# A macaron block with 4-bit weights: VectorE and DMA turn the down results and the convolution's rows

## The chip, the cores and the metric

The kernel runs on one core of one Trainium2 chip. The metric is the device time of one execution in microseconds (us), as the median of several runs. A separate execution, taken by the hardware profiler, gives the rows that are quoted below. PE is TensorE, DVE is VectorE, ACT is ScalarE, POOL is GpSimd, and SP is the engine that issues most DMAs.

## The reference

The input has 2048 tokens (2 x 1024) of 1024 channels in float32. The block is a feed-forward half step, a state-space convolution, and another feed-forward half step:

```python
x = x + 0.5 * ffn(layernorm(x))
x = x + s4(layernorm(x))
x = x + 0.5 * ffn(layernorm(x))

ffn(x) = (silu(x @ Wg) * (x @ Wu)) @ Wd     # 1024 -> 2752 -> 1024
W[k, n] = scales[k // 128, n] * (w4[k, n] - (z4[k // 128, n] + 1))   # 4 bits each
s4(u)  = causal convolution of u, along its last axis (1024), with a kernel K, plus D * u
```

K is made from the state-space parameters. The convolution runs along the channel axis, independently for each token, and the same K serves all tokens. So it can be written as products with triangular Toeplitz blocks, and the convolved axis has to stand on the partitions for that.

## The kernel before

**Jobs.** The 2048 tokens are cut into 4 blocks b of 512 (TB), and each block into 4 tiles t of 128 rows. Rows of x stand on partitions. A job is one feed-forward step of one block: `JOBS` (L1418) lists the eight as (b, k), where k = 1 is the first and k = 3 the second feed-forward: (0,1), (1,1), (0,3), (1,3), (2,1), (3,1), (2,3), (3,3). Job j runs `gate_up` and then `down`.

**Gate/up** (L727) has 64 steps: 8 waves over the intermediate columns by 8 groups g of 128 input channels. A wave has 6 units (3 column tiles by gate and up) in most waves, 4 in two and 5 in the last, and each unit holds one of the 8 PSUM banks. One step multiplies the group's weights by the block, with a high and a low part of x (two matmuls of 128x512 for each unit, L753). Since the scale differs from group to group, the accumulated bank is rescaled in place after every group: by ACT for even units (L723) and by DVE for odd ones (L725). The next group's products into that bank wait for it.

**Down** (L814) has 44 steps: 2 halves a of the output columns by 22 input tiles f. One step has 4 banks c (128 output channels each, 512 tokens wide) with two matmuls each (L825); banks c0 and c2 are rescaled by ACT, c1 and c3 by DVE. At f = 21 the result goes to four tiles y (L837, from `ypool`, which has 4 buffers). They hold output channels on partitions, so they are turned before they are added to x.

**Turning the down results.** `back(b, a, t)` (L843) takes a PSUM bank, makes four TensorE transposes of 128x128 (L847), one from each y, and DVE adds the bank to x (L849). For a = 0 these stand in steps 26 to 41 of the same down, for a = 1 in steps 0 to 3 of the next job's gate/up.

**The convolution** of the block that the job before finished (when k was 1) stands in the gate/up of jobs 1, 2, 5 and 6. For each of 4 tiles, `norm` makes normalized rows (L223), `swap` (`turn_whole`, L1193) turns them by eight transposes (L230) into PSUM and copies them to SBUF by ACT (L1201) and DVE (L1199), and `convolve` (L1137) makes sums on POOL (L1146 to L1148), small products in two halves with two banks each (L1151), and adds to x on DVE (L1181 to L1191).

**Other work beside it.** The next block's rows are normalized (L256), split by POOL and turned by DMA transposes (`turn_by_dma`, L258) during down. Weights are loaded as bytes on SP's queue four steps ahead (L685 in gate/up, L692 in down, 6 buffers) and cast by POOL three steps ahead (L701, 5 buffers).

**Order.** `at(up, s, f)` and `at(dn, d, f)` put a piece of work in front of step s of gate/up or d of down in the order of writing. A scheduler then orders each engine's instructions by its own estimate; `in_order_of_writing(f, engines)` holds f to the written order on the named engines. `bank()` gives out the 8 PSUM banks in rotation, `acc()` holds one until `give_back`.

Of the kernel before, what the change touches and what calls it, by code (L numbers as in the profile page):

```python
# [55 lines left out]
def macaron_s4_kernel(  # L56
# [785 lines left out]

    def back(b, a, t):  # L843

        ps = bank(f"pb_{b}_{a}_{t}")
        for c in range(4):
            nc.tensor.transpose(ps[:, bass.ts(c, P)], yT[a, c][:, bass.ts(t, P)], ident)  # L847
        part = x[b][t][:, bass.ts(a, 512)]
        nc.vector.tensor_tensor(part, part, ps, ALU.add)  # L849
# [570 lines left out]
    def fast():  # L1420
# [5 lines left out]
        for j, (b, k) in enumerate(JOBS):  # L1426
# [7 lines left out]
            if prev:  # L1434
                pb, pk = prev
                for t in range(NT):
                    at(up, t, lambda t=t: back(pb, 1, t))
                if pk == 1:
                    late = 34 if j == 1 else 0
                    at(up, 4, lambda: moments(pb, 2))  # L1440
                    at(up, 5, lambda: deviations(pb, 2))
                    s4x, s4n = {}, {}

                    def norm(t):
                        s4n[t] = normalized(pb, t)

                    def swap(t):
                        s4x[t] = turn_whole(s4n.pop(t), f"st_{pb}_{t}")
# [19 lines left out]
                    at(up, late + 28, save)  # L1468
                else:
# [6 lines left out]
                    at(up, 4, store)  # L1476
# [21 lines left out]
            if after:  # L1498
# [44 lines left out]
            at(dn, o, lambda: load_x(b, rows_of(u, b) if k == 1 else saved(b)))  # L1543
            for t in range(NT):
                at(dn, o + 5 + gap * t, lambda t=t: back(b, 0, t))
                if not after:
                    first_half = lambda t=t: store_half(t, 0, nc.sync)
                    at(dn, o + 6 + gap * t, first_half)
# [207 lines left out]
```

## Time and profile before

| | |
|---|---|
| median of 3 runs | 2097.34 us (2096.61 to 2097.39) |
| span of the profiled execution | 2095.8 us |
| granted TensorE clock, mean | 0.998 |
| PE busy | 2054.6 us |
| DVE busy | 1671.5 us |
| ACT busy | 1398.9 us |
| POOL busy | 1291.6 us |
| DMA packets | 239719, of which 98747 under 512 B |

The profiled execution has its span, from the first to the last instruction, as its own time; no device time stands beside it. It is 1.5 us under the median of the three runs, which had no profile. "Chain" means the chain of work that ended last, followed back from the last instruction to what released each step. A group is written as line, engine, operation, output and inputs with their shapes, count, then busy time and the mean of one in ns. The durations of neighbouring matmuls overlap, so the chain, not the mean, says what one adds.

### The profile page before, as it was taken

Reading aid. Unit: us, or ns where it says so; the run is one execution under the profiler, and the core shown is the slowest. Engines: PE = TensorE matmul, PEld = TensorE weight load, DVE = VectorE, ACT = ScalarE, POOL = GpSimd, SP = SyncE. Lnnn points to the kernel's source line nnn. Section 1 sums busy time; section 2 is a strip of 40 time slices with the busy share of each in tenths; the row PEclk is TensorE's granted clock in tenths of the full one; section 3 lists DMA queues with packets and bytes.
Section 4 is the critical chain, followed back from the end, with each engine's and each line's share of the span. In section 5 each row is a group of like instructions: output and inputs, shape, how many; then the busy total and the mean of one; then the engine's idle time right before and its main releaser. Section 6 shows DMA issues by size and latency. Waiting matters only on the chain.

```text
span 2095.8 us, 30242 instructions
## 1 busy us (share of the span) xinstructions
PE 2054.6 (98%) x9556; PEld 1410.6 (67%) x9556; DVE 1671.5 (80%) x2749; ACT 1398.9 (67%) x2185; POOL 1291.6 (62%) x1688
## 2 busy tenths in 40 slices
PE   6999999999999999999999999999999999999998
PEld 4555775677776578655876568675686766866576
DVE  8888887778888877797778878878788787777776
ACT  6777777746655776667667776547765467667775
POOL 5867758657754577555955568455684546845542
PEclk9999999999999999999999999999999999999999
DMA  4324321113411126211441124111151111531111
GB/s 144 119 85 146 111 66 54 36 56 74 110 39 55 32 53 170 72 31 36 122 137 37 31 51 126 44 51 32 46 130 37 51 39 35 133 128 36 33 35 60
DMA packets 239719, 151.03 MB, mean 72 GB/s; under 512 B 98747, under 2 KB 226596, under 8 KB 239550
## 3 DMA queue, kind: packets, MB, share of 16 engines
q1 hardware_dynamic: 238246, 146.60, 24.7%
q8 instruction: 78, 1.28, 0.3%
q10 hardware_dynamic: 1016, 1.82, 0.2%
q14 instruction: 91, 0.75, 0.1%
q0 software_dynamic: 288, 0.59, 0.1%
HBM read 104.45 MB, written 25.50 MB: 62 GB/s over the span
## 4 chain that ended last, share of the span: by engine, by line
PE 92%; DVE 4%; DMA 1%; ACT 1%; issue 1%; POOL 0%; SPq 0%; ACTq 0%; DVEq 0%; POOLq 0%
PE pg L753 56%; PE po L825 29%; PE pc L1151 3%; PE pb L847 1%; PE pb L1151 1%; DVE pg L725 1%; PE st L230 1%; DMA b<-wq 1%; ACT g L780 0%; DVE po L725 0%; DVE x L256 0%; DMA x<-in_L_attn_u_dram 0%; POOL q L608 0%; DVE hf L783 0%; PE pt L230 0%
## 5 line engine op out<-in xcount | busy, mean ns | idle before, releaser
L723 ACT ACTIVATE pg<-pg,rat 128x512 f32<-128x512 f32 x1240 | 787.5, 661 | 418.1 <-PE pg L753 415.9
L725 DVE TENSOR_TENSOR pg<-pg,rat 128x512 f32<-128x512 f32 x1168 | 776.6, 693 | 159.3 <-PE pg L753 153.4
L753 PE MATMUL pg<-xTh,w_up 128*128 128x512 f32 x2752 | 840.5, 435 | 1.1 <-DVE pg L725 0.7
L753 PE MATMUL pg<-xTl,w_up 128*128 128x512 f16 x2752 | 716.7, 382 | 11.6 <-DVE pg L725 5.6
L701 POOL CAST w_up<-b 128x768 fp32r<-128x768 int8 (+2 forms) x490 | 378.0, 777 | 504.6 <-PE pg L753 405.7
L753 PEld LDWEIGHTS pg<-xTh,w_up 128*128 128x128 f32 x2752 | 518.3, 189 | 175.9 <-DVE pg L725 12.2
L723 ACT ACTIVATE po<-po,ratd 128x512 f32<-128x512 f32 x660 | 431.8, 661 | 164.7 <-PE po L825 164.1
L825 PE MATMUL po<-hl,w_down 128*128 128x512 f32 x1344 | 530.5, 397 | 3.7 <-DVE po L725 3.6
L825 PE MATMUL po<-hh,w_down 128*128 128x512 f32 x1344 | 521.2, 390 | 0.0
L725 DVE TENSOR_TENSOR po<-po,ratd 128x512 f32<-128x512 f32 x620 | 430.4, 698 | 113.3 <-PE po L825 109.1
L753 PEld LDWEIGHTS <-w_up 128*128 128x128 bf16 x2752 | 228.4, 99 | 330.3 <-issue 151.0
L701 POOL CAST w_down<-bd 128x512 fp32r<-128x512 int8 x352 | 218.4, 624 | 158.5 <-PE po L825 90.4
L825 PEld LDWEIGHTS po<-hl,w_down 128*128 128x128 f32 x1344 | 251.2, 188 | 73.3 <-DVE po L725 12.2
L825 PEld LDWEIGHTS po<-hh,w_down 128*128 128x128 f32 x1344 | 252.6, 188 | 49.0
L787 POOL TENSOR_TENSOR hl<-hf,hh 128x512 fp32r<-128x512 f32 x168 | 217.9, 1297 | 8.0
L783 DVE SCALAR_TENSOR_TENSOR hf<-pg,rat,g 128x512 f32<-128x512 f32 x168 | 123.2, 749 | 49.3 <-ACT g L780 40.4
L780 ACT ACTIVATE g<-pg,rat 128x512 f32<-128x512 f32 x168 | 111.0, 687 | 48.5 <-PE pg L753 32.8
L785 POOL CAST hh<-hf 128x512 fp32r<-128x512 f32 x168 | 106.1, 632 | 55.0 <-PE pg L753 31.0
L282 POOL TENSOR_TENSOR lo<-x,hi 128x512 f16<-128x512 f32 x48 | 62.2, 1296 | 0.0
L187 DVE BATCH_NORM_STATS2 stats<-x 128x6 f32<-128x512 f32 x88 | 60.0, 682 | 0.5
L280 POOL TENSOR_TENSOR mid<-hi,top 128x512 bf16<-128x512 f32 x48 | 56.4, 1174 | 0.0
L296 POOL TENSOR_TENSOR xTh<-turned 128x512 fp32r<-128x512 bf16 x48 | 55.9, 1165 | 0.0
(216 smaller groups left out, 1104.2 us busy)
## 6 DMA issues: line engine op xcount, KB each, us to landing
b<-wq SPq DMA_DIRECT2D x319, 96.0 KB
bd<-wdq SPq DMA_DIRECT2D x336, 64.0 KB
x<-in_L_attn_u_dram SPq DMA_DIRECT2D x30, 512.0 KB
b<-wq SPq DMA_DIRECT2D x128, 64.0 KB
xs<-x SPq DMA_DIRECT2D x16, 512.0 KB
x<-xs SPq DMA_DIRECT2D x16, 512.0 KB
out_dram<-x SPq DMA_DIRECT2D x12, 512.0 KB
b<-wq SPq DMA_DIRECT2D x64, 80.0 KB
```

The lines of the kernel that those rows point to most:

```text
L187: nc.vector.bn_stats(stats[:, t, i, :], x[b][t][:, bass.ts(i, 512)])
L282: nc.gpsimd.tensor_tensor(lo[:, own], n[:, own], hi[:, own].bitcast(F32), ALU.subtract)
L701: nc.gpsimd.tensor_copy(t, b)
L723: nc.scalar.activation(dst, src, AF.Copy, scale=sc)
L725: nc.vector.tensor_tensor(dst, src, sc.to_broadcast([P, TB]), ALU.mult)
L753: nc.tensor.matmul(p, weights, (lo, hi)[k][:, g, :], start=(g == 0 and not done), stop=(g == GK - 1 and done), skip_group_check=True,)
L780: nc.scalar.activation(g, pg, AF.Silu, scale=rat[:, 2 * f, GK - 1 :])
L783: nc.vector.scalar_tensor_tensor(hf, pu, last, g, ALU.mult, ALU.mult)
L785: nc.gpsimd.tensor_copy(hi, hf)
L787: nc.gpsimd.tensor_tensor(lo, hf, hi.bitcast(F32), ALU.subtract)
L825: nc.tensor.matmul(ps[c], w[:, bass.ts(c, P)], part, start=(f == 0 and k == 0), stop=(f == NF - 1), skip_group_check=True,)
L1151: nc.tensor.matmul(dst, lhsT, rhs, start=start, stop=stop, skip_group_check=True)
```

## The change

Two uses of TensorE transposes go.

The down results: `blocks_out(a, cs)` transposes each y in place in blocks of 32x32 on DVE and writes it to a DRAM tile `y_dram[a]` (256 KB). `rows_in(b, a, t)` reads the rows of tile t back with four DMAs, one for each 32 partitions, each of 512 runs of 32 floats (128 B); the DMA's addresses put the blocks in their turned places. `back` then adds that tile to x, SBUF with SBUF. The last job's a = 1 keeps the products, under the name `back_by_products`. The writes stand at steps 23 and 24 of down (a = 0) and at steps 0 and 1 of the next gate/up (a = 1), held on DVE and SP; the reads follow at 26, 30, 34, 38 of down (29, 32, 35, 38 in job 0) and at 3 to 6 of gate/up, held on SP, and the adds at 29, 33, 37, 41 and at 5 to 8.

The convolution's rows: `norm` transposes the normalized tile in place on DVE (128x1024, blocks of 32x32) and writes 512 KB to one of two DRAM tiles; `swap` reads it with four DMAs of 1024 runs of 128 B. The convolution's steps move by two or three places (in job 1 two less, since `late` is 32 there), so that the way through DRAM lies between them; the moments, deviations and stores beside them move too.

```diff
+    y_dram = [dpool.tile([TB, 512], F32, tag=f"yz{a}", name=f"yz{a}") for a in range(NH)]
+    s_dram = [dpool.tile([P, HID], F32, tag=f"sz{i}", name=f"sz{i}") for i in range(2)]
+    Q = 32
+    def blocks_out(a, cs):
+        for c in cs:
+            y = yT.pop((a, c))
+            nc.vector.transpose(y, y)
+            nc.sync.dma_start(y_dram[a][bass.ts(c, P), :], y)
+    rows_back = {}
+    def rows_in(b, a, t):
+        r = ypool.tile([P, TB], F32, tag="y", name=f"yr_{b}_{a}_{t}")
+        src = y_dram[a].rearrange("(m j) (t b i) -> t b j m i", j=Q, b=P // Q, i=Q)[t]
+        for q in range(P // Q):
+            dst = r[bass.ts(q, Q), :].rearrange("p (m i) -> p m i", i=Q)
+            nc.sync.dma_start(dst, src[q])
+        rows_back[b, a, t] = r
     def back(b, a, t):
+        part = x[b][t][:, bass.ts(a, 512)]
+        nc.vector.tensor_tensor(part, part, rows_back.pop((b, a, t)), ALU.add)
+    def back_by_products(b, a, t):
...
                 pb, pk = prev
+                for i in range(2):
+                    out_ = lambda i=i: blocks_out(1, (2 * i, 2 * i + 1))
+                    at(up, i, lambda out_=out_: in_order_of_writing(out_, ET.DVE, ET.SP))
                 for t in range(NT):
-                    at(up, t, lambda t=t: back(pb, 1, t))
+                    in_ = lambda t=t: rows_in(pb, 1, t)
+                    at(up, 3 + t, lambda in_=in_: in_order_of_writing(in_, ET.SP))
+                    at(up, 5 + t, lambda t=t: back(pb, 1, t))
                 if pk == 1:
-                    late = 34 if j == 1 else 0
-                    at(up, 4, lambda: moments(pb, 2))
-                    at(up, 5, lambda: deviations(pb, 2))
-                    s4x, s4n = {}, {}
+                    late = 32 if j == 1 else 0
+                    at(up, 8, lambda: moments(pb, 2))
+                    at(up, 9, lambda: deviations(pb, 2))
+                    s4x = {}
                     def norm(t):
-                        s4n[t] = normalized(pb, t)
+                        n = normalized(pb, t)
+                        nc.vector.transpose(n, n)
+                        nc.sync.dma_start(s_dram[t % 2], n)
                     def swap(t):
-                        s4x[t] = turn_whole(s4n.pop(t), f"st_{pb}_{t}")
+                        s4x[t] = s = t4(f"st_{pb}_{t}").rearrange("p (c t) -> p c t", c=NC)
+                        src = s_dram[t % 2].rearrange(
+                            "(b i) (c a j) -> a i c b j", i=Q, a=P // Q, j=Q
+                        )
+                        for q in range(P // Q):
+                            dst = s[bass.ts(q, Q)].rearrange("p c (b j) -> p c b j", j=Q)
+                            nc.sync.dma_start(dst, src[q])
...
+                    pinned = lambda f, *e: lambda: in_order_of_writing(f, *e)
                     for t in range(NT):
-                        at(up, late + 8 + 4 * t, lambda t=t: norm(t))
-                        at(up, late + 10 + 4 * t, lambda t=t: swap(t))
-                        at(up, late + 12 + 4 * t, lambda t=t: conv(t))
-                        at(up, late + 13 + 4 * t, lambda t=t: next(parts[t], None))
-                    at(up, late + 27, lambda: moments(pb, 3))
-                    at(up, late + 28, lambda: deviations(pb, 3, LIFT))
+                        at(up, late + 10 + 4 * t, pinned(lambda t=t: norm(t), ET.DVE, ET.SP))
+                        at(up, late + 13 + 4 * t, pinned(lambda t=t: swap(t), ET.SP))
+                        at(up, late + 15 + 4 * t, lambda t=t: conv(t))
+                        at(up, late + 16 + 4 * t, lambda t=t: next(parts[t], None))
+                    at(up, late + 29, lambda: moments(pb, 3))
+                    at(up, late + 30, lambda: deviations(pb, 3, LIFT))
...
-                            d, where = 31 + 2 * t + half, up
+                            d, where = 32 + 2 * t + half, up
...
+            for i in range(2):
+                out_ = lambda i=i: blocks_out(0, (2 * i, 2 * i + 1))
+                at(dn, 23 + i, lambda out_=out_: in_order_of_writing(out_, ET.DVE, ET.SP))
             for t in range(NT):
-                at(dn, o + 5 + gap * t, lambda t=t: back(b, 0, t))
+                d = o + gap * t + (2 if j == 0 else 5)
+                in_ = lambda t=t: rows_in(b, 0, t)
+                at(dn, d, lambda in_=in_: in_order_of_writing(in_, ET.SP))
+                at(dn, d + 3, lambda t=t: back(b, 0, t))
...
         for t in range(NT):
-            back(b, 1, t)
+            back_by_products(b, 1, t)
```

More of the change, by code (lines that the diff above doesn't have):

```diff
@@ L1466, in save @@
                             nc.sync.dma_start(dst, x[pb][t])
-                    at(up, late + 28, save)
+                    at(up, late + 30, save)
                 else:
@@ L1474, in store @@
                         x.pop(pb)
-                    at(up, 4, store)
+                    at(up, 9, store)
             if j == 0:
@@ L1543, in fast @@
             at(dn, o, lambda: load_x(b, rows_of(u, b) if k == 1 else saved(b)))
+            for i in range(2):
+                out_ = lambda i=i: blocks_out(0, (2 * i, 2 * i + 1))
+                at(dn, 23 + i, lambda out_=out_: in_order_of_writing(out_, ET.DVE, ET.SP))
             for t in range(NT):
-                at(dn, o + 5 + gap * t, lambda t=t: back(b, 0, t))
+                d = o + gap * t + (2 if j == 0 else 5)
+                in_ = lambda t=t: rows_in(b, 0, t)
+                at(dn, d, lambda in_=in_: in_order_of_writing(in_, ET.SP))
+                at(dn, d + 3, lambda t=t: back(b, 0, t))
                 if not after:
                     first_half = lambda t=t: store_half(t, 0, nc.sync)
-                    at(dn, o + 6 + gap * t, first_half)
+                    at(dn, d + 4, first_half)
             gate_up(j, b, up)
```

## The prediction

> **What bounds the kernel now.** I read the busy shares first, then the chain that ended last, then this chain piece by piece in two stages, then rows and windows for prices.
>
> The page's head and chain:
>
> ```profile
> span 2095.8 us, 30242 instructions
> PE 2054.6 (98%) x9556; PEld 1410.6 (67%) x9556; DVE 1671.5 (80%) x2749; ACT 1398.9 (67%) x2185; POOL 1291.6 (62%) x1688
> PE 92%; DVE 4%; DMA 1%; ACT 1%; issue 1%; POOL 0%; SPq 0%; ACTq 0%; DVEq 0%; POOLq 0%
> PE pg L753 56%; PE po L825 29%; PE pc L1151 3%; PE pb L847 1%; PE pb L1151 1%; DVE pg L725 1%; PE st L230 1%; DMA b<-wq 1%; ACT g L780 0%; DVE po L725 0%; DVE x L256 0%; DMA x<-in_L_attn_u_dram 0%; POOL q L608 0%; DVE hf L783 0%; PE pt L230 0%
> ```
>
> PE is busy 98% and carries 92% of the chain, and both groups of transposes that the change removes (pb L847, st L230) stand in the chain under their own names. VectorE, which receives the work, is the next engine, at 80%.
>
> The chain piece by piece, in a down stage and in the gate/up of job 2 (start us, us, what):
>
> ```profile
> 540.10 7.30 PE po L825 x32
> 547.41 0.44 PE pb L847 x4
> 547.84 7.33 PE po L825 x32
> ...
> 594.97 0.87 PE st L230 x8
> 595.84 2.91 PE pg L753 x13
> ...
> 601.39 1.75 PE pc L1151 x12
> 603.15 0.22 PE pb L1151 x2
> ```
>
> PE has no gap around the transposes: 0.44 us for four, 0.87 for eight, then products at once. (32 products take 7.3 us, 0.228 each.) A group's mean duration of 275 ns is not its price, since starts overlap: the price is 0.11 us.
>
> **Removed.** 60 groups at L847 by 0.44 us = 26.4 us; 16 tiles at L230 by 0.87 us = 13.9 us. Sum 40.3 us of PE time on the path, where PE never waits long: job 2's gate/up took 188.6 us against some 185 of PE work. The page's L847 and L230 shares (1.4% and 0.7%, some 44 us) agree. Also gone are 16 copies on ACT (L1201, 586 ns) and 16 on DVE (L1199, 680 ns): both beside PE, at nothing, except that the DVE time pays for part of what comes.
>
> The Trainium skill, "TensorE: Matmul & The Clock Gate", Part 4, gives a PE transpose about 275 ns in a kernel; by that the 368 removed would be 101 us, and the chain's pieces overrule it.
>
> **Added on VectorE.** 60 transposes of 128x512 and 16 of 128x1024, an operation that this trace does not show. Bounds: below, the fastest DVE rows of these shapes (0.53 and 0.80 us); above, the same rows at their slowest:
>
> ```profile
> L256 DVE TENSOR_SCALAR x<-x,mv,r x56: 529/540/1480, 248.4 to 1714.4; 128x512 f32<-128x512 f32 x56
> L223 DVE TENSOR_SCALAR xn<-x,mv,r x16: 802/806/1719, 399.1 to 1646.4; 128x1024 f32<-128x1024 f32 x16
> L1199 DVE COPY st<-st x16: 677/680/683, 416.9 to 1663.7; 128x512 f32<-128x512 f32 x16
> L849 DVE TENSOR_TENSOR x<-x,pb x64: 674/677/690, 267.2 to 2088.5; 128x512 f32<-128x512 f32 x64
> ```
>
> I take the plain copy, 0.68 shown; queued back to back such operations follow at some 0.61 us (four L725 in 2.53). For 128x1024 I take 1.1, nearly twice the pitch. The back's add stays one DVE operation; it now reads SBUF twice instead of PSUM once. I leave it at 0.68, bounded by 0.53 and 1.48.
>
> *In down* (8 stages, half a=0): after y at step 21, two transposes each are pinned at steps 23 and 24. The window of one down stage:
>
> ```profile
> core 0: us, PE busy (x) PEld busy (x) DVE busy (x) ACT busy (x) POOL busy (x), PEclk, DMA share, GB/s
> 505.00:540.00 35.00, 35.00 (x160) 28.93 (x159) 26.92 (x40) 24.33 (x37) 31.10 (x42) 1.00 0.60 150
> 2010.00:2050.00 40.00, 40.00 (x178) 33.09 (x177) 30.05 (x44) 28.30 (x43) 16.18 (x26) 1.00 0.14 40
> ```
>
> DVE is idle 8.1 of 35 us: 0.42 us in each 1.82 us step. The burst is 4 x 0.61 = 2.4 us in two steps with 0.8 us spare, so c1 and c3 are rescaled 1.6 us late. The changed order lets PE take c0 and c2 of the next step first, which is 0.9 us of work; 0.8 us remains. 8 x 0.8 = 6.4 us. If PE's run-ahead covers all: 0. Without cover, with 1.48 us each: 8 x 5.1 = 41.
>
> *In gate/up* (7 stages, half a=1): the same burst in steps 0 and 1, of 2.7 us each, with three DVE rescales (2.1) in each, 0.6 spare; 1.2 us late, of which six open banks cover most. I take 0.3: 2.1 us (0 to 7 x 4.7 = 33). The 16 large ones replace 16 copies, +0.4 us each, in steps that have 0.6 spare: nothing (16 x 1.0 = 16 if the spare is gone).
>
> **Added on the queue and the DMAs.** 60 + 16 writes, 240 gathers of 512 runs and 64 of 1024 runs of 128 B: 188,000 packets beside the present 239,719. No row has 128-B runs between DRAM and SBUF. Nearest: L993 reads 2 x 1024 runs of 32 B, and both landed in some 2.5 us, 10 ns an engine and packet; the 512-B rows of bd cost 25 to 27 ns (3,470 packets, 13.7% of 16 engines in 2010 to 2050). I take 13.5, with 10 and 28 as ends. Four gathers of 512 runs are then 2048 x 13.5 / 16 = 1.7 us (1.3 to 3.6), a swap of 4096 runs 3.4 us (2.6 to 7.2). A back stands three steps of 1.82 us behind its gathers in down and two of 2.7 in gate/up, 5.4 us; each is hidden at the value taken, with about 2 us of latency added.
> The adds (L868) are a new wait of VectorE on a DMA: behind one that waits stand the rescales c1 and c3 of the step, and behind these PE's next products into the same banks, so a gather late by 1 us costs PE up to 1 us. The gathers in turn take the four y buffers, so SP holds them until the write of the block has landed (256 KB, issued two to three steps earlier, 3.6 us or more); behind SP then stand weight loads, with the lead named below. Both at nothing.
> SP issues take 0.32 to 0.57 us whatever the number of runs (L993: 427 and 572 ns). In gate/up the 16 gathers stand together ahead of the weight load b_12, 16 x 0.5 = 8 us; six byte buffers of 2.7 us keep some 14 us of loads ahead: nothing. In down four gathers and three DMA transposes stand ahead of bd_34, 4 x 0.5 + 3 x 1.25 = 5.8 us, and POOL, busy 31.1 of 35 us there, does not wait for long: nothing. If cover goes, it is up to 5 us a stage.
>
> The Trainium skill, "VectorE: DVE Perf Modes", The three transpose paths, warns that a plain DMA used as a strided transpose is 19 times slower than the crossbar. Here VectorE turns within blocks and DMA only moves 128-B runs, so I do not apply it; by it a tile's gathers would take tens of us and the kernel would run far over 2200. No run yet shows which.
>
> **Moved.** The static order of the changed program shows the largest loss. For jobs 2, 5 and 6 the convolution's products, written at gate/up steps 15 to 28, stand at 23 to 35, since the scheduler holds the gathers for slow; the banks they keep let only four of the six units run in steps 32 to 35, and the other two follow in 36 to 46. With four units, a rescale (0.7 us and handing over, 1.2 to 1.5 in all) is covered by three others, 3 x 0.45 = 1.35: about 0.3 us a step, and 1.5 more behind the x adds (L1181) that free the banks: 2.5 a stage, 7.5. In job 1 only two of four units run in steps 48 to 52: 0.9 us of work in each round trip of some 1.8, so 0.9 x 5 = 4.5, and 1.5 for the adds: 6. Sum 13.5 (0, if PE fills all, to 30, at twice these). In job 1's down the four normalizes also come together at step 1.5 instead of spread: 4 x 0.54, 2 us (0 to 6).
>
> **Sum.** 2095.8 - 40.3 + 6.4 + 2.1 + 13.5 + 2 = 2079.5 of span. The median is 1.5 above this profiled span (2097.34), so 2081 us.
>
> **The rivals.**
> *Full gain:* PE's run-ahead and spare banks cover bursts and moved products. For it: DVE has 20% idle in the whole, and the chain has waits of DVE of 4% only. Against: the four held units. 40.3 less some 6: 2063.
> *Back to where it was:* losses of 36 to 44 eat it up, for instance both the conv stages and the bursts at twice my price (44 to 48 with the rest): 2097.
> *VectorE becomes the bound (slower):* its transposes run at the slow end, as L256 and L223 do at times while POOL works on SBUF. Place: steps 22 to 24 of down and 0 to 1 of gate/up, where DVE has no slack left after 0.61 us each. Price: 0.87 us more each for 60, 52 us, and for 16 large ones 0.6, 10 us; 2081 + 62 = 2143. At half of this excess it is 2112. It decides from 0.27 us more for each (60 x 0.27 = 16), at about 0.88 us a transpose at pitch.
> *Gathers too slow (slower):* at 28 ns a packet a down stage with turning gets 4 x 3.6 = 14.3 us of DMA more in 35 where 0.60 is taken (1.01 together): the weights come late, 5 to 10 us in 8 stages: 2121 to 2161. Against: L993.
>
> **How the numbers follow.** Chances: forecast (2070 to 2092) 0.44, full gain (under 2070) 0.17, back to where it was 0.09, VectorE the bound 0.20, gathers too slow 0.10. A measurement can tell some 0.2% here, 4.2 us. Faster by more: the first two and a little of the third, 0.62; within: 0.08; slower: 0.30. The range leaves out the best tail of the full gain and the far part of the two slow rivals (together 2 in 10): 2062 to 2116. The likeliest side's own range is 2062 to 2092.
>
> **What would show it.** Right: L847 in 4 products only, st L230 gone, PE's busy time down by about 40 us and the span by 16; DVE transposes of 0.6 to 0.75 us; new PE idle under DVE po L725 near step 23 of each down and under DVE x L1181 in gate/up of jobs 1, 2, 5 and 6; weight casts not waiting for DMA. The VectorE rival: transposes over 0.88 us. The gather rival: backs (L868) or POOL casts waiting on DMA. The forecast is wrong if PE's idle does not grow (then 2060), or grows by over 40 us.

## The result and the profile after

The changed kernel takes 2133.32 us (median of 4 runs, 2132.22 to 2136.22), beside 2096.98 us for the kernel before in the same series. The ratio is 1.0178, with a 95% interval of 1.0164 to 1.0193: 36 us slower, where 16 us faster was forecast. The profiled execution took 2136.22 us, with a span of 2134.4; it is the slowest of the four, 2.9 us above their median, so differences read from its stages are some 2 us larger in all than that of the medians.

The head of the page and the chain that ended last:

```profile
span 2134.4 us, 30145 instructions
PE 2049.8 (96%) x9188; PEld 1357.3 (64%) x9188; DVE 1724.1 (81%) x2809; ACT 1389.4 (65%) x2169; POOL 1297.3 (61%) x1688
PE 74%; DVE 6%; POOL 1%; issue 1%; DMA 1%; ACT 1%; SPq 0%; DVEq 0%; POOLq 0%; ACTq 0%
PE pg L753 46%; PE po L825 23%; PE pc L1178 3%; DVE pg L725 1%; PE pb L1178 1%; DVE x L868 1%; DVE x L256 1%; DVE y L851 1%; DVE po L725 0%; ACT pg L723 0%; POOL w_down L701 0%; DVE stats L187 0%; DVE y L725 0%; DVE hf L783 0%; DMA bd<-wdq 0%
```

PE issues 368 matmuls less, as planned, but its busy time falls by 4.8 us only. The shares of the chain are shares of the span, and here they add up to 84%: the chain could be followed back to 340.1 us only. PE has 74 of these 84, some 88%, where it had 92 of 99. pb L847 and st L230 are gone from the chain, x L868 and y L851 of DVE are new in it. The groups of the gate/up products say why the busy time is no measure here (busy us, mean ns, idle before):

```profile
L753 PE MATMUL pg<-xTh,w_up 128*128 128x512 f32 x2752 | 890.0, 447 | 8.5 <-ACT pg L723 3.0
L753 PE MATMUL pg<-xTl,w_up 128*128 128x512 f16 x2752 | 736.8, 384 | 32.7 <-POOL w_up L701 20.5
```

The same 5504 products were busy for 1557.2 us before (840.5 and 716.7) and are now for 1626.8. Part of it is the granted clock (mean 0.993, before 0.998), part perhaps short waits that the records count into the matmuls; no run parts the two. Idle time in front of them was 12.7 us and is 41.2.

So I measured by stages instead: from one job's first gate/up product to its first down product, and from there to the next job's first product. Difference to the kernel before, in us; 1.76 us of transposes went from every stage but job 0's gate/up, and 3.48 more from the gate/up of jobs 1, 2, 5 and 6 (four tiles by 0.87):

| job | 0 | 1 | 2 | 3 | 4 | 5 | 6 | 7 |
|---|---|---|---|---|---|---|---|---|
| gate/up | 4.0 | 22.2 | -0.5 | -1.1 | -1.2 | 0.5 | 0.4 | 3.6 |
| down | 0.5 | 4.9 | -0.4 | 0.4 | 1.3 | 1.3 | 0.5 | -0.7 |

Counted from the first gate/up product, the last product of down is 35.8 us late; the part behind it is 3.1 us longer, and the part ahead of the first 0.3 shorter. With the removed work added back, the losses are: gate/up of job 1 27.4, of jobs 2, 5 and 6 16.0 together, of job 7 5.4, of job 0 4.0, of jobs 3 and 4 1.3; the eight downs 21.9; the two ends 2.8. Together 79, of which the prediction had priced 24.

The operations themselves, from the answers by source line (duration min/median/max in ns):

```profile
L851 DVE STREAM_TRANSPOSE y<-y x60: 657/680/705, 252.6 to 2086.0; 128x512 f32<-128x512 f32 x60
...
L1478 DVE STREAM_TRANSPOSE xn<-xn x16: 1226/1234/1239, 434.5 to 1697.5; 128x1024 f32<-128x1024 f32 x16
...
L868 DVE TENSOR_TENSOR x<-x,yr x60: 679/684/1623, 272.4 to 2125.8; 128x512 f32<-128x512 f32 x60
```

The transposes cost about what was estimated and are even: the VectorE rival, which needed 0.88 us, did not occur. The add, which now reads SBUF twice, reaches 1.62 us. The waits (who waited for whom: us, times, longest):

```profile
POOL w_up L701 <- DMA b<-wq: 38.5, 8, 11.9
...
PE pg L753 <- POOL w_up L701: 20.5, 6, 7.8
POOL w_down L701 <- DMA bd<-wdq: 19.4, 11, 3.8
...
PE po L825 <- DVE po L725: 8.7, 13, 1.3
```

In the kernel before, the same four were 22.9, 2.2, 3.5 and 3.6 us. So PE now waits for weight casts of POOL, and POOL waits longer for weight loads. These are queue waits, in engines that the prediction had at "nothing"; "weight casts not waiting for DMA" was one of its signs of being right, and POOL casts waiting on DMA one of the gather rival's.

**Where the order is late.** I followed one block through job 5's gate/up in both traces (us from that job's first product):

| | before | after |
|---|---|---|
| rows written to DRAM | - | 1.8 to 5.4 |
| gathers issued | - | 7.7 to 15.7 |
| adds of a = 1 to x | 1.8 to 10.7 | 15.8 to 35.8 |
| last operation of the deviations | 23.0 | 44.3 |
| first normalized row | 23.2 | 45.1 |
| its gathers issued | - | 53.9 to 56 |
| first product of the convolution | 35.7 | 65.8 |
| last tile of the convolution begins | 89.4 | 115.9 |

The last gather is issued 20 us before the last add. No add kept VectorE waiting for its gather: VectorE stood idle in front of none of the 60 for more than 0.03 us. The answer for their line (L868) has nothing under its first heading:

```profile
its engine sat idle before it (us, times) until:
who waited for it (us, times):
```

The program's static order puts the adds there: on VectorE rescales stand in front of them. That the scheduler holds the way through DRAM for long is the likely reason; no run shows it. Moments, deviations, normalized rows and convolution all follow some 21 to 30 us later.

### The profile page after: what moved, and what is told of

Same layout as the page of the kernel before. It is cut to its first block, busy times and chain, and to the rows that moved or that the text cites. A ratio compares the mean times of both kernels' runs of the same rounds, so it can differ in the third digit from the quotient of the medians.

```text
span 2134.4 us, 30145 instructions
## 1 busy us (share of the span) xinstructions
PE 2049.8 (96%) x9188; PEld 1357.3 (64%) x9188; DVE 1724.1 (81%) x2809; ACT 1389.4 (65%) x2169; POOL 1297.3 (61%) x1688
## 3 DMA queue, kind: packets, MB, share of 16 engines
q8 instruction: 75, 1.23, 0.2%
## 4 chain that ended last, share of the span: by engine, by line
PE 74%; DVE 6%; POOL 1%; issue 1%; DMA 1%; ACT 1%; SPq 0%; DVEq 0%; POOLq 0%; ACTq 0%
PE pg L753 46%; PE po L825 23%; PE pc L1178 3%; DVE pg L725 1%; PE pb L1178 1%; DVE x L868 1%; DVE x L256 1%; DVE y L851 1%; DVE po L725 0%; ACT pg L723 0%; POOL w_down L701 0%; DVE stats L187 0%; DVE y L725 0%; DVE hf L783 0%; DMA bd<-wdq 0%
## 5 line engine op out<-in xcount | busy, mean ns | idle before, releaser
L753 PE MATMUL pg<-xTh,w_up 128*128 128x512 f32 x2752 | 890.0, 447 | 8.5 <-ACT pg L723 3.0
L753 PE MATMUL pg<-xTl,w_up 128*128 128x512 f16 x2752 | 736.8, 384 | 32.7 <-POOL w_up L701 20.5
L825 PE MATMUL po<-hh,w_down 128*128 128x512 f32 x1344 | 514.6, 391 | 0.0
L701 POOL CAST w_down<-bd 128x512 fp32r<-128x512 int8 x352 | 223.1, 638 | 170.5 <-PE po L825 91.3
```

The lines of the kernel that those rows point to most:

```text
L701: nc.gpsimd.tensor_copy(t, b)
L753: nc.tensor.matmul(p, weights, (lo, hi)[k][:, g, :], start=(g == 0 and not done), stop=(g == GK - 1 and done), skip_group_check=True,)
L825: nc.tensor.matmul(ps[c], w[:, bass.ts(c, P)], part, start=(f == 0 and k == 0), stop=(f == NF - 1), skip_group_check=True,)
```

## The experiments

My theory after the result was **lateness**: the adds of a = 1 stand too late in the static order, and everything written behind them collides with what was tuned to stand at another place. Rivals: the convolution's place in PE's order (the prediction's own largest term), VectorE's added work, and DMA contention. Ratios are to the kernel before in the same series. Each expectation was written before its run. In e6 and e9 the second normalization of jobs 2, 5 and 6 stands in front of the convolution's last adds, so there it works on unfinished rows, and their times are not those of a full version.

**e3: job 1 without rows.** Only the turning of a = 1 in job 1's gate/up goes back to products.

```diff
+                if j == 1:
+                    for t in range(NT):
+                        at(up, t, lambda t=t: back_by_products(pb, 1, t))
-                for i in range(2):
+                for i in range(2) if j > 1 else ():
...
-                for t in range(NT):
+                for t in range(NT) if j > 1 else ():
```

> Only the a = 1 half that is turned in job 1's gate/up goes back to TensorE products (steps 0 to 3); all else as changed. Theory O (order): in the changed program POOL's written order in job 1 puts the casts of weights 9, 10 and 11 behind six GpSimd operations that wait for later work, and PE stands still 4.2 and 7.9 us for them, with the clock halved after; steps 4 to 13 of that stage lose 17.7 us. With the products POOL's order is again that of before, so 2133 less 16: 2113 to 2120 us, and no wait of PE on w_up over 1 us in job 1. Rival C (contention: the new DVE adds, transposes and 128-byte runs slow their neighbours everywhere): one of 15 groups undone gives 2 to 5 us, 2128 to 2132 us.

Measured: 2115.89 us, 1.0085 (1.0069 to 1.0102); 17.4 us back by one of 15 uses. The stage falls from 22.2 to 7.1. PE's timeline of the changed kernel in this stage shows the two gaps (start, us, what, idle before and releaser):

```profile
325.15 1.46 PE L753 MATMUL pg<-xTl,w_up 128*128 128x512 f16 x3 [4.21 <-POOL w_up L701]
...
340.18 1.46 PE L753 MATMUL pg<-xTl,w_up 128*128 128x512 f16 x3 [7.85 <-POOL w_up L701]
```

and POOL's timeline beside it, what POOL did instead of the casts:

```profile
318.06 0.61 POOL L785 CAST hh<-hf 128x512 fp32r<-128x512 f32 x1 [4.38 <-DVE hf L783]
...
324.27 1.59 POOL L701 CAST w_up<-b 128x768 fp32r<-128x768 int8 x2
331.87 1.48 POOL L957 TENSOR_TENSOR s_cos<-s_dr 128x512 f32<-128x512 f32 x1 [6.01 <-DVE s_sin L950]
...
339.31 2.36 POOL L701 CAST w_up<-b 128x768 fp32r<-128x768 int8 x3
```

POOL waits 6 us for VectorE's sine, in front of a cast that PE needs. The tables of the convolution kernel (L950 to L961) stand in job 1 only, so this is the one job where late adds and tables can meet on VectorE. The windows of the stage, first of the changed kernel:

```profile
core 0: us, PE busy (x) PEld busy (x) DVE busy (x) ACT busy (x) POOL busy (x), PEclk, DMA share, GB/s
294.00:324.00 30.00, 25.54 (x111) 14.77 (x109) 23.27 (x52) 22.95 (x36) 10.47 (x12) 1.00 0.53 138
324.00:354.00 30.00, 21.00 (x74) 11.90 (x75) 23.82 (x39) 12.92 (x21) 15.71 (x18) 0.77 0.16 36
```

then of e3:

```profile
294.00:324.00 30.00, 29.46 (x136) 17.73 (x134) 27.71 (x69) 23.77 (x39) 15.63 (x17) 1.00 0.28 83
324.00:354.00 30.00, 30.00 (x135) 17.48 (x133) 25.26 (x42) 24.15 (x40) 24.94 (x29) 1.00 0.25 72
```

PE issues 74 matmuls instead of 135 in the second window, and behind the gaps its clock is lower (0.77).

**e11: POOL's order in job 1.** The changed kernel, with job 1's weight casts (steps below 24), the first hh and hl, and the tables held on POOL in the order of writing.

```diff
+        elif j == 1 and stage == "up" and s < 24:
+            in_order_of_writing(lambda: nc.gpsimd.tensor_copy(t, b), ET.Pool)
...
-                    piece = lambda: in_order_of_writing(lambda: next(tables, None), ET.DVE)
+                    piece = lambda: in_order_of_writing(
+                        lambda: next(tables, None), ET.DVE, ET.Pool
+                    )
```

> The changed kernel with POOL's work in job 1's gate/up held in the order of writing as far as step 23 (casts of weights, the split of the products, the tables); the gathers of a = 1 stay. The casts of weights 9 and 10 then stand ahead of the six split operations again, and those of 11 to 14 between the tables. Theory O (it is the order on POOL that starves PE in steps 8 to 11): as with job 1's products, 12 to 16 us less, 2117 to 2121 us, PE waits for w_up under 2 us in job 1. Rival Q (the weight bytes themselves are late behind the 16 gathers on SP): the casts wait for DMA, and the time stays at 2129 to 2134 us.

Measured: 2130.54 us, 1.0155 (1.0140 to 1.0171); the expectation fell. Casts are in time now, and PE waits for VectorE in the same place:

```profile
338.74 1.01 PE L755 MATMUL pg<-xTl,w_up 128*128 128x512 f16 x2 [8.75 <-DVE pg L727]
```

The rescales stand behind the 13 small operations of the deviations (330.7 to 338), and seven of these took 0.71 to 1.11 us each beside POOL's tables and casts, where such operations took 0.14 to 0.17 with POOL quiet. By these rows some 4.8 of the 7.3 us are lengthening, an estimate. So POOL's order is not what starves PE: with the casts in time, VectorE's late sequence does, and the tables beside it stretch it.

**e4: the stores of job 7 later.** These four stores (L1514) read x behind the late adds and stand on SP in front of weight loads.

```diff
-                    at(up, 9, store)
+                    at(up, 16, store)
```

> Only the four stores of a finished block move from step 9 to step 16 of gate/up (jobs 3, 4 and 7 have none or one such; job 7 shows the stall). Theory O: in job 7 SP stands 18 us on the adds into x (L868) with the next weight loads behind it, and PE waits 4.1 us at step 13, with a clock step after: 5.8 us come back, 2127 to 2129 us. Rival C: the loads are late since the 16 gathers and their traffic hold the queue; moving the stores gives nothing, 2132 to 2134 us.

Measured: 2126.9 us, 1.0138 (1.0117 to 1.0158), as expected (0.1 us under the range); job 7's gate/up goes from 3.6 to -2.1. In the changed kernel SP's timeline shows the wait,

```profile
1898.53 18.34 SPq L1514 DMA_DIRECT2D out_dram<-x  x4
1917.29 2.85 SPq L685 DMA_DIRECT2D b<-wq  x6
```

18 us in which SP issues four stores, one behind each late add, and no weight load. PE's gap follows:

```profile
1921.79 0.82 PE L753 MATMUL pg<-xTl,w_up 128*128 128x512 f16 x3 [4.08 <-POOL w_up L701]
```

**e1 and e2: the two uses apart.** e1 keeps the rows of the down results and turns the convolution's rows by `turn_whole` at the changed steps; e2 keeps only the convolution's way through DRAM.

```diff
e1: in norm and swap
+                        s4n[t] = normalized(pb, t)
+                        s4x[t] = turn_whole(s4n.pop(t), f"st_{pb}_{t}")
e2: in gate/up and down
+                        at(up, t, lambda t=t: back_by_products(pb, 1, t))
+                at(dn, d + 3, lambda t=t: back_by_products(b, 0, t))
```

> The convolution's rows turned by TensorE again, at the changed steps; the down results by VectorE and DMA as changed. The swap alone measured 26 us over before. If the two parts add up, this is 2133 less 26, 2105 to 2110 us, nearly all of it in job 1's casts (15 to 17) and job 7's store (6), with the rest of the stages gaining 0 to 2 us each. If the parts hinder one another (the gathers of the swap behind those of the rows), it is under 2100.

> All down results are turned by TensorE as before (in the steps of before); only the convolution's rows go by VectorE blocks and DMA, at the changed steps. Theory O: no burst in down (15 of the 22 us lost there come back beyond the transposes' own price), POOL's order in job 1 and the store as before; what stays is the late convolution. 2097 less 13.9, plus 16 in jobs 2, 5, 6 and about 8 in job 1: 2104 to 2111 us. Rival C with the swap's traffic (64 gathers of 1024 runs) as the main load: 2118 or more.

Measured: e1 2132.14 us, 1.0159 (1.0143 to 1.0175); e2 2123.42 us, 1.0125 (1.0108 to 1.0142). Both fell; both are much slower than expected, and e2 lies in the range of its rival (the swap's traffic as the main load, 2118 or more). Its trace does not show that traffic at work, though: POOL waits 22.5 us for gate/up's weight loads, 22.9 before, and PE for no gather. Together (36.2 and 25.8 us over the stages) they cost more than the whole change (35.8): the parts do not add. In the gate/up of jobs 2, 5 and 6, e1 is 5.2, 4.8 and 4.9 us late and e2 6.0, 3.9 and 5.0. Either use alone makes the convolution late: its first product in job 5 stands at 47.2 us in e1 and 51.6 in e2, against 35.7 before and 65.8 with both. The lateness adds up, but the loss does not: with the removed products added back, e1 loses 6.5 to 7.0 us in each of the three stages, e2 7.4 to 9.5, and both together only 4.7 to 5.7. So it is not the lateness by its length that costs, but what the late work meets. In e1 the convolution's turning is the old one, so its loss comes through the late adds or through the steps, which stay moved by two or three places; no run parts these two. (e2 also loses 6.6 in job 1's gate/up and 3.7 in its down, where it turns no rows.)

**e5 and e6: the convolution's place on PE.** The prediction had its largest loss there. e5 holds the convolution's products, and the gate/up products of the steps around them, on PE where they are written; e6 does it five steps later. In job 1 of e6 (late = 28) the products stand one step later and the normalization and gathers four steps earlier.

```diff
-                        at(up, late + 15 + 4 * t, lambda t=t: conv(t))
+e5:                     at(up, late + 15 + 4 * t, pinned(lambda t=t: conv(t), ET.PE))
+e6:                     at(up, late + 20 + 4 * t, pinned(lambda t=t: conv(t), ET.PE))
```

> The convolution's products and the gate/up products of the steps beside them are held in the order of writing on PE (steps 15 to 28 in jobs 2, 5 and 6, 47 to 60 in job 1), so that they stand at 15, 16, 19, 20, ... and not up to eight steps later, and all six units run in every step. Theory O: jobs 2, 5 and 6 get back about 5 us each and job 1 some 6: 2133 less 21, 2108 to 2117 us. Rival C (the gathers are slow, and the scheduler was right to put the products late): PE waits on DMA ahead of L1178 and the time is 2133 or more.

> As the run with the convolution's products held in order on PE, but five steps later: at 20, 21, 24, 25, ... in jobs 2, 5 and 6, and in job 1 norm and swap four steps earlier with the products at 48, 49, 52, ... The turned rows of the first tile were there some 54 us after the start of gate/up, which is step 20. Theory O2 (the late, bunched place of the products costs PE, and the way through DRAM needs 11 us from the normalized row to the landed tile, which step 15 does not leave): no wait of PE on st over 1 us, jobs 2, 5 and 6 gain 4 to 5 us each and job 1 some 6: 2133 less 18 to 20, 2110 to 2118 us. Rival W (the loss of these stages is in the DVE adds and transposes themselves, whatever the place): 2128 to 2134 us.

Measured: e5 2165.51 us, 1.0332 (1.0311 to 1.0353); e6 2128.04 us, 1.0141 (1.0124 to 1.0158). e5 fell badly, and its group line says why:

```profile
L1184 PE MATMUL pc<-near,st 128*128 128x256 f32 (+1 forms) x256 | 52.8, 354 | 45.1 <-DMA st<-sz 45.1
```

PE waits 45 us for the gathers. In job 5 the row was normalized at 1391.4 us, written from 1393.6, gathered by issues at 1396.3 to 1399.1 and landed at about 1402, some 11 us in all; the written place asked for it earlier. So the scheduler's late place was needed. Five steps later, jobs 5 and 6 gain 3.3 and 2.4 us over the changed kernel and job 2 loses 4.0. The 5.3 us of the median are under a third of what was expected, and they lie in the range of the rival, that the loss is not in the place.

**e7 and e8: the two small terms of down.** e7 copies each gathered tile of a = 0 to PSUM on ACT before the add; e8 spreads the four transposes over steps 22 to 25.

```diff
e7:
+        if a == 0:
+            row, ps = ps, bank(f"pr_{b}_{a}_{t}")
+            nc.scalar.copy(ps, row)
e8:
-            for i in range(2):
-                out_ = lambda i=i: blocks_out(0, (2 * i, 2 * i + 1))
-                at(dn, 23 + i, lambda out_=out_: in_order_of_writing(out_, ET.DVE, ET.SP))
+            for i in range(4):
+                out_ = lambda i=i: blocks_out(0, (i,))
+                at(dn, 22 + i, lambda out_=out_: in_order_of_writing(out_, ET.DVE, ET.SP))
```

> In down alone, ACT copies the gathered rows to a PSUM bank and DVE adds x and the bank, so that the add reads SBUF once, as before. In the changed kernel the add of two SBUF tiles takes 0.68 us with no GpSimd operation running at its start and up to 1.62 with one, and GpSimd's next operation is longer too; PE then waits 1 to 1.5 us at steps 30 to 36 of several downs. Theory X (the add and GpSimd exclude one another): the adds in down take 0.68 us, the waits go: 4 to 8 us less, 2125 to 2129 us. Rival: the wait in down is the late weight bytes behind the gathers on SP; then the adds get shorter and the time stays, 2132 to 2136 us with 32 more ACT copies.

> In down, one transpose and one write stand at each of the steps 22, 23, 24 and 25, not two at 23 and two at 24. The burst cost 0.83 us at steps 24 and 25 of every down. Theory B (DVE has 0.42 us spare in a step, so one transpose a step is nearly covered): 0.5 to 0.8 us less for each of 8 downs, 4 to 6 us: 2127 to 2129 us. Rival: the last write is later, the gathers with it, and a later add gives it back: 2132 to 2135 us.

Measured: e7 2128.32 us, 1.0141 (1.0124 to 1.0158); e8 2127.08 us, 1.0140 (1.0121 to 1.0158). Both as expected, 5 and 6.2 us. By stages the eight downs together are 2.4 us shorter in e7 and 6.0 in e8, so half of e7's gain stands in stages that its edit does not touch and is not shown to be its own. In the changed kernel, steps 23 to 26 of a down (jobs 1 to 7) took 1.1 to 1.2 us more than the steps ahead of them, by the starts of PE's products; spread, the transposes still cost some 0.5 to 0.7 in steps 22 to 27. The downs of jobs 1 and 3 to 7 are 0.5 to 1.3 us shorter in e8, those of jobs 0 and 2 up to 0.3 longer. What e7 takes away is in the chain of waits of the changed kernel, in job 4's down:

```profile
1325.36 1.41 DVE x L868
...
1326.80 0.69 DVE stats L187
1327.49 0.61 DVE po L725
```

PE waits for that rescale. In e7 the adds from PSUM stay at 0.69 us, and those still from SBUF (a = 1) do not:

```profile
L872 DVE TENSOR_TENSOR x<-x,pr x32: 674/687/690, 270.7 to 2118.5; 128x512 f32<-128x512 f32 x32
L872 DVE TENSOR_TENSOR x<-x,yr x28: 680/683/1500, 314.3 to 1910.6; 128x512 f32<-128x512 f32 x28
```

**e9, e10, e12: mended versions.** e9 joins e3, e4, e6, e7 and e8. e10 is e9 with the convolution's rows through DRAM only in jobs 5 and 6, and its normalization later. e12 starts from the kernel before and turns rows only where no convolution follows: in every down (spread, added from PSUM) and in the gate/up of jobs 3, 4 and 7.

```diff
e12, against the kernel before:
+                through = pk == 3
...
-                    at(up, 4, store)
+                    at(up, 16, store)
```

> All five together: job 1's a = 1 half by products, the stores at step 16, the convolution held at the later steps, the adds in down from PSUM, and the transposes in down one a step. If the causes add up, 2133 less 17, 6, 19, 6 and 5: 2080 us (2075 to 2090), which is faster than before. If they overlap or another wait comes last: 2095 to 2105 us.

> What the runs say is worth keeping: job 1's a = 1 half and the convolution's rows of jobs 1 and 2 by TensorE; those of jobs 5 and 6 by VectorE and DMA, with the products held five steps later and the next normalization behind them; stores at step 16; one transpose a step in down; the adds in down from PSUM. From the stages of the runs before: jobs 1 and 2 at 0, jobs 3 to 7 at 1 to 2.6 us each less in gate/up and 0 to 1.2 in down, 10 to 12 us in all: 2085 to 2090 us against 2097, faster than before. Rival: DVE and SP are so full that each freed PE cycle is lost at the next burst: 2095 to 2100 us.

> The kernel before, with the new way only where no convolution follows: a = 0 in every down (one transpose a step, adds from PSUM), a = 1 in the gate/up of jobs 3, 4 and 7 (stores at step 16). The convolution and all its steps are those of before. Theory L (the loss outside job 1's casts and job 7's store comes from the adds of a = 1 landing some 25 us later and pushing the convolution behind them): jobs 1, 2, 5 and 6 keep the gate/up time of before, the rest gains 1 to 2 us in each gate/up and 0 to 1 in each down: 2087 to 2092 us against 2097, faster. Rival D (the loss is in DVE and SP in down): downs are longer than before and it comes to 2096 to 2102 us.

Measured: e9 2102.55 us, 1.0021 (1.0011 to 1.0030); e10 2102.09 us, 1.0020 (1.0011 to 1.0029); e12 2099.39 us, 1.0001 (0.9992 to 1.0010). All three are far better than the change and none reaches its expectation, 7 to 13 us above its upper end; e9 and e12 lie in the ranges named for the other case (parts that overlap; downs longer than before). I had added gains of parts that are not independent. In e12 the gate/up stages did what was expected, -0.1 to 0.3 us in jobs 1, 2, 5 and 6 and -1.1 to -2.2 in jobs 3, 4 and 7, and the downs did not. And a down that turns rows does not gain the 1.76 us of its transposes: in e12 four of the downs are 0.7 to 1.2 us shorter than before the change, and the other four 1.2 to 2.1 longer.

**e14 and e15: the lateness tested by itself.** e14 is e12 with rows also in the gate/up of jobs 5 and 6, where the moments and deviations stand four steps later and the convolution and the second normalization nine, so that the static order and the data agree. e15 is e14 with job 0's down by products and the second normalization two steps earlier.

```diff
-                through = pk == 3
+                through = j > 2
-                    late = 34 if j == 1 else 0
+                    late = 34 if j == 1 else 0 if j == 2 else 9
-                    at(up, 4, lambda: moments(pb, 2))
-                    at(up, 5, lambda: deviations(pb, 2))
+                    at(up, 8 if j > 2 else 4, lambda: moments(pb, 2))
+                    at(up, 9 if j > 2 else 5, lambda: deviations(pb, 2))
```

> As the run before it, and a = 1 of jobs 5 and 6 as well goes through DRAM; the convolution (turned by TensorE) and what follows it stand nine steps later there, behind the late adds, so that nothing has to catch up. Theory L: the lateness as such costs nothing once the order fits it, and each of the two gate/up stages keeps its 1.5 us of saved products where the run with the rows alone lost 4.8: 2 to 4 us under the run e12_small. Rival: the rows' traffic or the adds beside GpSimd cost PE in these stages wherever the convolution stands: 4 to 9 us over e12_small.

> As e14_rows_late_conv, with job 0's a = 0 half by TensorE again, since its down, where DVE also prepares weights, was 1 to 2 us longer than before in the last runs, and with the second normalization in jobs 5 and 6 two steps earlier, out of the short steps 40 to 47 where it cost 1.7 us. If both come back: 3 us under e14_rows_late_conv, some 0.2 to 0.25% under before (ratio 0.9975 to 0.998), just clear of it. If the gain is lost again elsewhere: ratio 0.999 to 1.000.

Measured: e14 2097.12 us, 0.9998 (0.9989 to 1.0007), 2.3 under e12. The number is as expected, but not its place: the gate/up of jobs 5 and 6 stands at 0.4 and 1.1 us against before, in e12 at 0.3 and 0.3, and the two intervals overlap. e15 2098.61 us, 1.0001 (0.9991 to 1.0010), no gain, so its expectation fell. In e14's job 5 nothing is lost through step 33: the stage stands 1.57 us ahead of the kernel before there, of 1.76 possible, where e1 with the same rows stands 4.2 behind. In job 6 it is 0.96 ahead, and e1 4.3 behind. This is the most direct test of the theory: the same gathers and adds, with the dependent work written later, cost little or nothing up to there. Then 1.75 us is lost in steps 40 to 43; e15's chain shows what there:

```profile
1451.10 1.25 DVE x L256
1452.35 1.20 DVE pg L725 x2
1453.55 0.91 DVE x L256
```

the normalizations, 0.53 to 0.54 us where POOL is quiet, lengthened, in front of rescales that PE waits for.

**e16 and e17: the last down's stores.** Left over were some 3 us behind the last product. In the changed kernel's last down, SP's timeline is:

```profile
2099.37 0.34 SPq L1451 DMA_DIRECT2D out_dram<-x  x1
2099.76 2.09 SPq L862 DMA_DIRECT2D yr<-yz  x4
...
2109.36 0.36 SPq L1451 DMA_DIRECT2D out_dram<-x  x1
2109.78 2.09 SPq L862 DMA_DIRECT2D yr<-yz  x4
2119.37 0.36 SPq L1451 DMA_DIRECT2D out_dram<-x  x1
2119.77 2.11 SPq L862 DMA_DIRECT2D yr<-yz  x4
```

The store of a tile waits for its add, and the gathers of the next tile stand behind the store: four ways through DRAM one after the other, 10 us each. The span then ends with an add of rows, the last operation of the chain:

```profile
2125.89 0.60 DVE x L868
```

e16 (from e14) and e17 (from the changed kernel) write these stores at step 42:

```diff
-                    at(dn, d + 4, first_half)
+                    at(dn, 42, lambda t=t, f=first_half: f(t))
```

> The version with rows in every down and in the gate/up of jobs 3 to 7, with the convolution's steps nine later, and one edit: in the last down the four stores of the first half (L1454) are written at step 42, behind the last gathers, and not one step behind each add. Theory (the last stores on SP hold the gathers): in that version a store waits on SP for its add, and the gathers of the next tile stand behind it; they are issued at 2062.5, 2073.5 and 2080.0 us of the profiled run, and the last add (2084.62) comes after the last products. With the edit the four groups of gathers follow each other within some 15 us, the part after the last product of down shrinks by 3 us to what it was before the change, and the median falls from 0.9998 to some 0.9984 of before (0.9975 to 0.9992), 2094 to 2097 us beside 2097 to 2099. Rival (what is long there is VectorE's own queue or the write of the last block): the adds still end after the products, and the ratio stays within 0.0005 of 0.9998.

> The changed kernel with the same one edit: the last down's four stores of the first half at step 42. Theory (these stores hold the gathers): the last operation of the chain is then an add of the products, not an add of rows (2125.89 us in the changed kernel's profile), the part after the last product of down is 2 to 3 us shorter, and the median is 2130 to 2132 us beside the changed kernel's 2133.3. Rival: no change, 2132 to 2134.

Measured: e16 2093.91 us (2090.84 to 2096.87, 12 runs) beside 2098.1, ratio 0.9981 (0.9973 to 0.9990); e17 2131.87 us, 1.0163 (1.0148 to 1.0178). Both as expected; e17's 1.5 us under the changed kernel are not clear of the noise, since the intervals overlap, but its last operation is an add of products again and its part behind the last product 2.0 us shorter. In e16 the same part of SP's timeline is

```profile
2050.40 4.04 SPq L861 DMA_DIRECT2D yr<-yz  x8
2054.53 0.43 SPq L692 DMA_DIRECT2D bd<-wdq  x1
2055.01 2.02 SPq L861 DMA_DIRECT2D yr<-yz  x4
...
2059.15 2.02 SPq L861 DMA_DIRECT2D yr<-yz  x4
```

16 gathers in 11 us. The part behind the last product was 3.6 us longer than before the change in e14 and is 0.6 us shorter in e16. e16 is the fastest version here, 4.2 us under the kernel before. It removes 52 groups at 0.44, 22.9 us of PE work, so it still loses 18.7 of it.

## Why the prediction was wrong

**Removed, right.** In e14's job 5, where the dependent work was moved along, 1.57 of the 1.76 us per four groups arrive. From one convolution tile's first product to the next one's it took 16.99 us in e6 and 17.87 before, 0.88 less where 0.87 was taken for the transposes. (Job 2's gate/up, read as 188.6 us, is 188.3 by the starts of its products; nothing hangs on it.)

**Sizes on VectorE, nearly right.** 0.680 us shown for the transposes (0.68 estimated) and 0.60 at pitch (0.61). The large ones took 1.23 shown, where 1.1 was taken. The rival that decided at 0.88 us did not occur: the transposes never passed 0.705.

**Packets, right.** The 188,500 packets of 128 B took 13.5 ns on average, the value taken. The Trainium skill, "VectorE: DVE Perf Modes", The three transpose paths, warns of a factor of 19 for strided DMA transposes with a large innermost stride; with blocks turned first and runs of 128 B, no run here shows it. The rival of slow gathers, with its price by 28 ns a packet, is out too.

**Bursts, a little under.** 1.1 to 1.2 us in a down of jobs 1 to 7, where 0.8 was taken; e8's downs are 6.0 us shorter with the transposes spread, and 0.5 to 0.7 a stage stays.

**The add, underpriced.** It was left at 0.68 with 1.48 as the upper end. 33 adds that began while an operation of POOL ran took 1.12 us on average, up to 1.62; 20 with POOL quiet took 0.681. Price by e7: 5 us in the median, 2.4 in the downs that it edits.

**The failed step.** "Each is hidden at the value taken, with about 2 us of latency added": the way through DRAM was priced by the transfer time against the three and two steps at which the adds are *written*, 5.4 us in gate/up. The adds of a = 1 do not stand there. They stand 16 to 36 us into the stage, and the prediction, which followed the static order for the convolution, gave this no price. Its bound of 1 us of PE for 1 us of late gather was a bound of the wrong thing: no add kept VectorE waiting for a gather; its place was late.

What that term became: job 1's gate/up, 27.4 instead of 6 and 0.3 (e3: the stage is 15.1 shorter without the rows; e11: it is no single queue); jobs 2, 5 and 6, 16.0 instead of 7.5 and 0.9 (e1, e2: either use alone loses more; e14: with the dependent work moved it is 0.2 us through step 33 in job 5 and 0.8 in job 6). Of job 1's 27.4, the rows account for 15.1 and the 1.76 of products that came back with e3; the other 10.6 are there without rows, with the convolution's way, priced at 6. The forecast had jobs 2, 5 and 6 at 2.5 each for another reason, units held by the banks. e5 shows that the place itself was needed, since the data come about 11 us after the row's normalization begins.

**"Both at nothing", wrong for SP.** The queue was checked for what stands ahead of b_12 and bd_34. Not checked were SP's stores that wait for a late add: 18 us in job 7 (e4: 6.4 us) and four serial ways through DRAM in the last down (e17: 2 us less behind the last product, 1.5 in the median, within the noise). In job 7 it was not the count of issues that held the weight load, as feared, but an issue that waits.

**The downs** were priced at 6.4, and 2 for job 1, and lost 21.9. Of it e8 finds 6.0 and e7 2.4, by stages. Job 1's down lost 6.7; e2, which turns no rows there, is still 3.7 us over the kernel before, so what the convolution's way leaves in this down is nearer 4 than 2. Some 9 us remain; 5 or so of them are what the transposes still cost when they are spread, and the rest is not attributed.

**What stays open.** What is left of job 1's loss in e3 (7.1 and 5.0 us). Why a down in e16 is only 0.7 to 1.1 us shorter than before the change in jobs 2, 3, 6 and 7, and longer in the others: late bd loads behind SP's gathers and VectorE's adds both stand in e14's chain of waits, and no run parts them. Job 0's gate/up, which the change does not touch, stands from -1.0 to 4.3 us against before in the profiles of these versions, so a difference of this size in one stage proves nothing by itself.

## What to carry to other kernels

Here a step through DRAM cost by its place in the static order, not by its bytes: list, for each consumer, where the scheduler puts it, and move everything that hangs on it along, before pricing the transfer. On an in-order DMA queue, look at each issue that waits for a late engine, and at the loads behind it. The parts of this change did not add up, so undo one use at a time and measure by stage.

## What the runs showed of the hardware

An add of two SBUF tiles took 0.68 us with POOL quiet and up to 1.62 while POOL worked; the same add with one operand in PSUM stayed between 0.674 and 0.690 in e7, and the 32x32 transposes were not lengthened (0.657 to 0.705, 37 of the 60 beside an operation of POOL). The Trainium skill, "SBUF — State Buffer", SBUF: two separate sides, describes an exclusive lock between VectorE with two SBUF inputs and POOL; these rows agree with it. The small operations of the deviations took 0.14 to 0.17 us with POOL quiet and 0.7 to 1.1 beside POOL's tables and casts in job 1.

At gaps on PE of 2.0 to 7.9 us, the granted clock of the changed kernel stood at half speed in blocks of 3.4 us or a multiple: 23.9 us in all ahead of the last down product's end (10.2 of it beginning inside the gap of 7.85 us in job 1). Before the change it was 3.4 us, at no such gap, and in e14 none, though PE has a gap of 3.2 us there. In job 1 the gaps of 4.21 and 7.85 us put the stage some 16 us back, so such a gap can cost more than its own length.
